# Attention on one core: the next unit's q and k projections in three parts behind the values, the first unit's in front of a branch

## The chip, the cores and the metric

The kernel runs on one core of a Trainium2 chip as one program. The metric is device time in microseconds (us), lower is better. A core has five engines with queues of their own that run side by side and wait for each other through semaphores: TensorE (matrix products, PE in the profile; its weight loads are PEld), VectorE (DVE), ScalarE (ACT), GpSimd (POOL) and SyncE (SP), which issues the transfers.

## What is computed

The reference is a chain of eight sublayers on 64 sequences of 64 tokens with 256 features; each pair is a conditioning and a mixer, and the mixer's output is added to x:

```python
x = x + _L0_attn_ref(_L0_cond_ref(x, cond, ...), query_proj, key_proj, value_proj, output_proj)
x = x + _L0_ffn_ref(_L0_cond2_ref(x, cond, weight), ...)
x = x + _L1_attn_ref(_L1_cond_ref(x, cond, Wx, Wh, b), ...)
x = x + _L1_ffn_ref(_L1_cond2_ref(x, cond, ...), Wg, W1, W2, W3)
```

The change touches the first line alone: a conditioned scan, and behind it a softmax attention inside each sequence with 16 heads of key width 16 and value width 64.

## The kernel before

The program is a row of stages on the same engines: the conditioned scan, attention, a quantised feed-forward (`ffn0`), a recurrent layer (`rnn`), a selective scan (`mamba`) and two mixtures of experts. While the first stages compute, SyncE's queue fills and packs tables in device memory for the mixtures.

The scan leaves its result `cs` with 64 channels for one half of the tokens on partitions 0 to 63 and for the other half on 64 to 127. Attention never forms the scan's output projection; it is folded into the weights: `Wqkv` (L375) gives q and k, and the values are folded into the output weights, so that the "values" of a token are the 64 scan channels themselves, turned round and kept in `rows`, and the output weights are `M`. `attention` (L310) makes `M` by `value_weights` (L297), loads a number that says whether a bias of the output projection is other than zero, and branches on it (L323, L324). The branch's body computes the bias's share with the same code; with the inputs of this case it is jumped over. Each engine passes the branch by itself, and the first instructions behind it wait for what was made in front of it. Behind the branch stands the main call of `attend`.

`attend` (L342) runs over 8 units of 512 tokens (256 of each half). A unit has four steps, for `i` in 0, 1 and `h` in 0, 1, each with 2 sequences of one half. It uses these pieces:

- `project(u, v, i)` (L369): with `i` 0 it makes q of unit `u`, with `i` 1 k. Four products go to two banks of PSUM, the memory that TensorE writes (the trace has two matmul rows for each product of this type, so eight). Then ScalarE reads them out. For q these are 16 activations (L382), since the heads of a bank are separated by four masks; for k four (L379).
- `scores(v, h, i)` (L390): products of k and q into two banks (L399), on VectorE a maximum (L404) and its subtraction (L405), on ScalarE the exponential E (L411), on VectorE its sum (L413) and reciprocal (L414), on GpSimd the scaling (L415).
- `values` (L418): products of E with `rows` into two banks (L424), and two copies to `oT` on ScalarE (L426).
- `project_out` (L428): a generator in four pieces of four products of `oT` and `M` (L433), with an addition to x on VectorE behind each second piece (L437).

PSUM in this stage is four names (`ps`, `s`, `acc`, `out`) of two banks each. A name's bank is given again when its reader is done with it, so the k projection can only be made when ScalarE has read q out of the `ps` banks.

`follow` (L444) makes one piece of an earlier unit's output and the values of an earlier step; with three steps in `late`, values run two steps behind scores. The loop at L455 sets the order: the scores of the step, one piece of other work, the next unit's q (second step) and k (third step), and `follow`. The "other work" is `keys`, which fills `rows` by 16 transposes and four copies on ScalarE (L331 to L336), then the ternary weights of `ffn0`, made on VectorE in pieces of up to 2.68 us (L511 to L518), a few squares and sums, and last a reciprocal square root (L100). The first unit's q and k are made behind the branch, before the loop.

A scheduler of the language lays each engine's instructions in an order of its own near that of the code, so a lump of activations can be split round an exponential; within an engine they then run strictly in that order.

Of the kernel before, what the change touches and what calls it, by code (L numbers as in the profile page):

```python
# [13 lines left out]
F32 = mybir.dt.float32  # L14
BF16 = mybir.dt.bfloat16
I32 = mybir.dt.int32
AF = mybir.ActivationFunctionType
# [4 lines left out]
P = 128  # L22
B, L, D = 64, 64, 256
NT = B * L
CH = 512
# [42 lines left out]
@contextmanager  # L68
def pairs_of_banks(g):

    before = g.psum
    with g.tc.tile_pool(name="pairs", bufs=2, space=PSUM) as g.psum:
        yield
    g.psum = before


def bank(g, shape=(P, CH), dt=F32, tag="ps"):
    tag = g.tag or tag
    return g.psum.tile(list(shape), dt, tag=tag, name=tag)
# [28 lines left out]
def evict(nc, i, out, in_):  # L108

    if i % 2:  # L110
        nc.scalar.copy(out, in_)
    else:
        nc.vector.tensor_copy(out, in_)
# [183 lines left out]
def value_weights(g, w, v, out, scale=1.0):  # L297


    nc = g.nc  # L300
    for i in range(0, w.H // 2, 2):
        ps = bank(g, (P, 2, D), tag="acc")
        for j in range(2):
            for r in range(2):
                rows = slice(r * L, (r + 1) * L)
                nc.tensor.matmul(ps[rows, j, :], v(i + j, rows), w.Wout[rows, i + j, :], start=True, stop=True)
        nc.vector.tensor_scalar(out[:, i : i + 2, :], ps, scale, None, ALU.mult)


def attention(g, wa, cs, beside, close_banks):  # L310

    nc, tc = g.nc, g.tc
    cs2 = cs.rearrange("p b l -> p (b l)")
    p_keys, close_keys = scoped(tc, "keys")
    M = p_keys.tile([P, wa.H // 2, D], F32, name="M")
    rows = p_keys.tile([P, NT // CH, 2, P], F32, name="keys")  # L320
    value_weights(g, wa, lambda i, r: wa.Wv[r, i, :], M)
    close_banks()
    (some,) = nc.values_load_multi_w_load_instructions(wa.any, min_val=0, max_val=D)[1]  # L323
    with tc.If(some > 0), tc.tile_pool(name="bias", bufs=1) as kp:  # L324
        ones = kp.tile([P, P], F32, name="ones")
        nc.vector.memset(ones, 1.0)
        c = kp.tile([P, wa.H // 2, D], F32, name="c")
        bv = lambda i, r: wa.bv[r, i : i + 1].to_broadcast([L, L])
        attend(g, wa, cs2, lambda u, i: ones, c, iter([lambda: value_weights(g, wa, bv, c, 1.0 / L)]), [])

    def keys():  # L331
        for i in range(NT // CH // 2):
            ps = bank(g, (P, 2, 2, P), tag="acc")
            for j in range(4):
                nc.tensor.transpose(ps[:, j // 2, j % 2], cs2[:, ts(i * 4 + j, P)], g.ident)
            evict(nc, 1, rows[:, ts(i, 2)], ps)  # L336

    attend(g, wa, cs2, lambda u, i: rows[:, u, i], M, chain((keys,), beside[0]), beside[1])
    close_keys()


def attend(g, wa, cs2, keys, M, beside, last):  # L342

    nc, tc = g.nc, g.tc
    H = wa.H
    HK = H * wa.K
    UT = CH // 2  # L350
    UB = CB // 2
    NU = NT // CH
    xh = g.xT.rearrange("p k (h t) -> p k h t", h=2)
    half = lambda i: slice(i * L, (i + 1) * L)
    with (
        tc.tile_pool(name="at2", bufs=2) as p2,
        tc.tile_pool(name="at3", bufs=3) as p3,
        pairs_of_banks(g),
    ):

        def unit():
            v = SimpleNamespace()

            v.q = p2.tile([P, 2, 2, UB, 4, L], F32, name="q")
            v.k = p2.tile([P, 2, 2, UT], F32, name="k")
            v.o = p2.tile([P, H // 2, 2, UT], F32, name="oT")
            return v

        def project(u, v, i):  # L369

            ps = [bank(g, (P, 2, UT)) for _ in range(2)]
            for hg in range(2):
                for h in range(2):
                    W = wa.Wqkv[half(h), i * HK + hg * P : i * HK + (hg + 1) * P]
                    nc.tensor.matmul(ps[h][:, hg, :], W, cs2[half(h), ts(u, UT)], start=True, stop=True)  # L375
            for h in range(2):
                for hg in range(2):
                    if i:
                        nc.scalar.activation(v.k[:, hg, h, :], ps[h][:, hg, :], AF.Identity, bias=wa.bqk[:, 1, hg : hg + 1])  # L379
                        continue  # L380
                    for j in range(4):
                        nc.scalar.activation(  # L382
                            v.q[:, hg, h, :, j, :],
                            ps[h][:, hg, :].rearrange("p (b l) -> p b l", l=L),
                            AF.Identity,
                            bias=wa.bq[:, hg, j : j + 1],
                            scale=wa.mask[:, j : j + 1],
                        )

        def scores(v, h, i):  # L390

            E = p3.tile([P, H, L], F32, name="E")
            mx = p2.tile([P, H], F32, name="mx")
            ps = [bank(g, (P, 2, 4, L), tag="s") for _ in range(2)]
            for hg in range(2):
                for r in range(2):
                    for j in range(2):
                        b = i * 2 + j
                        nc.tensor.matmul(  # L399
                            ps[r][half(j), hg], v.k[half(r), hg, h, ts(b, L)], v.q[half(r), hg, h, b], start=True, stop=True  # L400
                        )
            for r in range(2):
                m = mx.rearrange("p (hg r i) -> p r hg i", r=2, i=4)[:, r]
                nc.vector.tensor_reduce(m, ps[r], AX.X, ALU.max)  # L404
                nc.vector.tensor_tensor(  # L405
                    E.rearrange("p (hg r i) n -> p r hg i n", r=2, i=4)[:, r],
                    ps[r],
                    m.unsqueeze(3).to_broadcast([P, 2, 4, L]),
                    ALU.subtract,
                )  # L410
            nc.scalar.activation(E, E, AF.Exp)  # L411
            z = p2.tile([P, H], F32, name="z")
            nc.vector.tensor_reduce(z, E, AX.X, ALU.add)  # L413
            nc.vector.reciprocal(z, z)  # L414
            nc.gpsimd.tensor_mul(E, E, z.unsqueeze(2).to_broadcast([P, H, L]))  # L415
            return E

        def values(u, v, h, i, E):  # L418
            ps = [bank(g, (P, H // 2, L), tag="acc") for _ in range(2)]
            Er = E.rearrange("p (o r) n -> p r o n", r=2)  # L420
            s = keys(u, i)
            for r in range(2):
                for j in range(2):
                    nc.tensor.matmul(ps[j][half(r)], s[half(j), half(h)], Er[half(j), r], start=True, stop=True)  # L424
            for j in range(2):
                nc.scalar.copy(v.o[:, :, h, ts(i * 2 + j, L)], ps[j])  # L426

        def project_out(u, v):  # L428

            for k in range(KD):  # L430
                ps = bank(g, (P, 2, UT), tag="out")
                for o in range(H // 2):
                    nc.tensor.matmul(ps, M[:, o, ts(k, P)], v.o[:, o], start=(o == 0), stop=(o == H // 2 - 1))  # L433
                    if o == H // 4 - 1:
                        yield
                x = xh[:, k, :, ts(u, UT)]
                nc.vector.tensor_add(x, x, ps)  # L437
                yield


        late = []
        out = deque()

        def follow():  # L444
            for _ in islice(chain.from_iterable(out), 1):
                pass
            u, v, h, i, E = late.pop(0)
            values(u, v, h, i, E)
            if h and i:
                out.append(project_out(u, v))  # L450

        nxt = unit()
        for i in range(2):
            project(0, nxt, i)
        for u in range(NU):  # L455
            now, nxt = nxt, unit() if u + 1 < NU else None
            for i in range(2):
                for h in range(2):
                    late.append((u, now, h, i, scores(now, h, i)))
                    for piece in islice(beside, 1):  # L460
                        piece()
                    if nxt and i != h:
                        project(u + 1, nxt, i)
                    if len(late) > 2:
                        follow()
        for piece in chain(beside, last):
            piece()
        while late:
            follow()
        for _ in chain.from_iterable(out):  # L470
            pass
# [1610 lines left out]
```

## Time and profile before

| what | value |
|---|---|
| median of 10 runs | 2931.24 us (2927.79 to 2934.86) |
| profiled execution | 2930.42 us, its span 2928.5 us |
| TensorE busy | 2435.9 us, 83% of the span |
| VectorE, ScalarE, GpSimd busy | 60%, 48%, 45% |
| mean granted clock of TensorE | 0.909 |
| attention, from the branch to its last product | about 147 to 425 us |

The profile is one execution. A timeline lists instructions by start, with consecutive ones of a kind merged: the time beside the start is from the first one's start to the last one's end, `x8` is the number of rows, and the brackets hold the idle time of the engine before them and whose work ended it. A windows view gives busy time by engine in a stretch and the clock that TensorE was granted in it (1.00 is full speed).

Around the branch, VectorE writes the last part of `cs` from 146.20 to 146.89 us. Inside attention the busy times of 150 to 412 us are, on ScalarE, 60.1 us for the 128 activations of q, 34.7 us for the 64 copies to oT, 34.5 us for the 32 exponentials and 14.2 us for the 32 of k; on VectorE, 41.4 us for the subtractions, 41.1 us for the maxima, 39.0 us for the sums; on GpSimd, 61.6 us for the scaling.

### The profile page before, as it was taken

Reading aid. Unit: us, or ns where it says so; the run is one execution under the profiler, and the core shown is the slowest. Engines: PE = TensorE matmul, PEld = TensorE weight load, DVE = VectorE, ACT = ScalarE, POOL = GpSimd, SP = SyncE. Lnnn points to the kernel's source line nnn. Section 1 sums busy time; section 2 is a strip of 40 time slices with the busy share of each in tenths; the row PEclk is TensorE's granted clock in tenths of the full one; section 3 lists DMA queues with packets and bytes.
Section 4 is the critical chain, followed back from the end, with each engine's and each line's share of the span. In section 5 each row is a group of like instructions: output and inputs, shape, how many; then the busy total and the mean of one; then the engine's idle time right before and its main releaser. Section 6 shows DMA issues by size and latency. Waiting matters only on the chain.

```text
span 2928.5 us, 34738 instructions
## 1 busy us (share of the span) xinstructions
PE 2435.9 (83%) x12134; PEld 1716.6 (59%) x12148; DVE 1758.1 (60%) x2955; ACT 1413.7 (48%) x2406; POOL 1306.6 (45%) x1117
## 2 busy tenths in 40 slices
PE   4879997778857778888788888868987899999996
PEld 4533334447624455555455555546865678888885
DVE  0555547882169988898987879894344343323332
ACT  1465627774367575858465666643322222222220
POOL 0022225541067677777667777772745451111110
PEclk9978997889666999999999999989999999999998
DMA  9999610001021212121211222222786856555655
GB/s 232 367 363 340 207 25 8 19 22 55 15 65 65 79 62 76 62 76 62 76 55 69 80 76 84 79 94 68 228 281 215 309 203 247 205 204 186 221 184 181
DMA packets 183075, 406.04 MB, mean 139 GB/s; under 512 B 25312, under 2 KB 89056, under 8 KB 177520
## 3 DMA queue, kind: packets, MB, share of 16 engines
q1 hardware_dynamic: 169456, 366.80, 37.2%
q0 software_dynamic: 13440, 36.98, 3.3%
q8 instruction: 97, 1.59, 0.2%
q14 instruction: 82, 0.67, 0.1%
HBM read 280.76 MB, written 144.98 MB: 145 GB/s over the span
## 4 chain that ended last, share of the span: by engine, by line
PE 43%; DVE 19%; ACT 9%; issue 7%; POOL 5%; DMA 2%; SPq 0%; DVEq 0%; POOLq 0%; ACTq 0%
DVE hb L1000 11%; PE ps L1586 11%; PE acc L1484 7%; DVE hb L1002 3%; PE ps L1553 2%; PE yp L1016 2%; PE mq L1722 2%; PE mq L1738 2%; PE mp L897 2%; DVE xc L842 1%; PE ps L736 1%; PE ps L619 1%; POOL hb L961 1%; PE acc L736 1%; PE ps L1594 1%
## 5 line engine op out<-in xcount | busy, mean ns | idle before, releaser
L961 POOL TENSOR_TENSOR hb<-dx,Bn 128x1024 f32<-128x1024 f32 x256 | 601.6, 2361 | 261.6 <-PE yp L1016 255.1
L1000 DVE TENSOR_TENSOR_SCAN hb<-dA,hb 128x512 f32<-128x512 f32 x512 | 602.8, 1209 | 32.7 <-ACT dA L968 30.2
L968 ACT ACTIVATE dA<-delta,A 128x504 f32<-128x504 f32 x512 | 344.3, 683 | 305.4 <-DVE hb L1000 302.7
L1016 PEld LDWEIGHTS yp<-ident,hb 128*128 128x128 f32 x2048 | 268.0, 152 | 182.3 <-issue 143.8
L1002 DVE TENSOR_TENSOR hb<-hb,cb 128x1024 f32<-128x1024 f32 x256 | 312.1, 1219 | 83.0 <-PE cb L913 66.1
L1586 PE MATMUL ps<-gxT,w 128*128 128x256 f32 (+1 forms) x1600 | 325.1, 362 | 0.8 <-DVE gxT L1461 0.8
L1586 PEld LDWEIGHTS ps<-gxT,w 128*128 128x128 f32 x1600 | 276.9, 191 | 47.0 <-issue 12.1
L1016 PE MATMUL yp<-ident,hb 128*128 128x128 f32 x2048 | 302.2, 292 | 0.0
L1722 PE MATMUL mq<-x,moe_s 128*128 128x256 f32 x896 | 248.8, 410 | 49.1 <-ACT up L1729 28.4
L1268 POOL DMA_INDIRECT ffn_y<-gy,to x72 | 69.4, 964 | 457.7 <-ACT gy L1486 445.7
L1722 PEld LDWEIGHTS mq<-x,moe_s 128*128 128x128 f32 x896 | 168.2, 203 | 113.7 <-ACT up L1729 37.1
L1590 DVE TENSOR_TENSOR gh<-gs,ps 128x256 f32<-128x256 f32 (+1 forms) x200 | 78.8, 394 | 220.0 <-ACT gs L1589 219.7
L913 PE MATMUL cb<-parts,pick 80*128 80x512 bf16 x256 | 105.4, 412 | 112.6 <-DVE hb L1002 97.5
L1484 PE MATMUL acc<-w,gh 128*128 128x256 f32 (+1 forms) x864 | 187.6, 387 | 0.0
L1589 ACT ACTIVATE gs<-ps 128x256 f32<-128x256 f32 (+1 forms) x200 | 72.6, 363 | 232.4 <-PE ps L1586 227.1
L1486 ACT ACTIVATE gy<-acc,wt 128x256 f32<-128x256 f32 x152 | 67.1, 473 | 241.0 <-PE acc L1484 231.5
L415 POOL TENSOR_TENSOR E<-E,z 128x1024 f32<-128x1024 f32 x32 | 61.6, 1926 | 244.7 <-DVE z L414 169.4
L1484 PEld LDWEIGHTS acc<-w,gh 128*128 128x128 f32 (+1 forms) x864 | 145.6, 189 | 29.9 <-issue 12.8
L433 PE MATMUL out<-oT,M 128*128 128x512 f32 x256 | 129.8, 655 | 1.5 <-ACT oT L426 1.5
L1738 PE MATMUL mq<-moe_s,sh 128*128 128x256 f32 x448 | 116.7, 399 | 6.6 <-ACT up L1729 6.6
L1268 POOL DMA_INDIRECT moe_y<-gy,to x80 | 77.2, 966 | 82.0 <-ACT gy L1486 63.3
L1738 PEld LDWEIGHTS mq<-moe_s,sh 128*128 128x128 f32 x448 | 83.8, 197 | 42.5 <-issue 20.3
(462 smaller groups left out, 4506.2 us busy)
## 6 DMA issues: line engine op xcount, KB each, us to landing
w<-ffn_w SPq DMA_DIRECT2D x40, 2176.0 KB, 9.1
Bn<-B SPq DMA_DIRECT2D x128, 512.0 KB, 3.7
moe_x<-fill SPq DMA_DIRECT2D x130, 260.0 KB, 5.6
ffn_x<-fill SPq DMA_DIRECT2D x129, 260.0 KB, 5.9
w<-moe_w SPq DMA_DIRECT2D x48, 512.0 KB, 4.8
ffn_w<-in_ffn_W_dram SPq DMA_DIRECT2D x16, 640.0 KB, 8.9
gx<-moe_x SPq DMA_DIRECT2D x32, 260.0 KB, 4.9
gx<-ffn_x SPq DMA_DIRECT2D x32, 260.0 KB, 9.2
```

The lines of the kernel that those rows point to most:

```text
L433: nc.tensor.matmul(ps, M[:, o, ts(k, P)], v.o[:, o], start=(o == 0), stop=(o == H // 2 - 1))
L913: nc.tensor.matmul(t, pick[:, n : n + 1].to_broadcast([rows, P]), v.parts, start=True, stop=True)
L961: nc.gpsimd.tensor_mul(hb, vs[c].dx[p], Bn[:, n % NB, :].unsqueeze(1).to_broadcast([P, PI, CH]))
L968: nc.scalar.activation(decays[s][i][:, :, 1:], seq(vs[c].delta[p][:, i, :])[:, :, 1:], AF.Exp, scale=w.A[:, p * PI + i, n : n + 1],)
L1000: ins = nc.vector.tensor_tensor_scan(h, dA[i].rearrange("p b l -> p (b l)"), h, 0.0, ALU.mult, ALU.add)
L1002: ins = nc.vector.tensor_tensor(hb, hb, cb.unsqueeze(1).to_broadcast([P, PI, CH]), ALU.mult)
L1016: nc.tensor.matmul(yp[i][:, t, :], hb[:, i, ts(t, P)], g.ident, start=(n == 0 and t == 0), stop=(n == S - 1 and t == CH // P - 1), is_tran ...
L1268: i = self.g.nc.gpsimd.indirect_dma_start(out=self.y, out_offset=bass.IndirectOffsetOnAxis(ap=to, axis=0), in_=y, in_offset=None)
L1484: nc.tensor.matmul(po[s], h, w, start=(i == 0), stop=(i == n - 1))
L1586: nc.tensor.matmul(ps[:, j, :], v.w12[:, k, ts(j * (full + 1) + i, P)], v.xT[:, k, :], start=(k == 0), stop=(k == KD - 1))
L1722: nc.tensor.matmul(ps[:, i % 2, :], w[:, k, ts(i, P)], xu[:, k, :], start=(k == 0), stop=(k == KD - 1))
L1738: nc.tensor.matmul(ps[:, t, :], h[:, i, ts(t, P)], self.s2[:, i, :], start=(i == 0), stop=(i == NS - 1))
```

## The change

`project` and the unit's tiles become functions of their own. `project` takes a `part`: 0 makes q of the first group of heads, 1 q of the second, 2 makes k. Parts 0 and 1 each take two banks and use half of each. In the loop a part stands behind `follow`, in steps one, two and three of a unit. The tiles of q and k are two fixed sets in the outer pool in place of a rotating pair. The first unit's three parts and the filling of `rows` move in front of the branch; the branch's body, where it is taken, makes the first unit's parts again at its end. The other pieces of work each come one step earlier, since `keys` is no longer one of them.

```diff
     rows = p_keys.tile([P, NT // CH, 2, P], F32, name="keys")
+    units = [unit(p_keys, i) for i in range(2)]
+    for part in range(3):
+        project(g, wa, cs2, 0, units[0], part)
     value_weights(g, wa, lambda i, r: wa.Wv[r, i, :], M)
+    for i in range(NT // CH // 2):
+        ps = bank(g, (P, 2, 2, P), tag="acc")
+        for j in range(4):
+            nc.tensor.transpose(ps[:, j // 2, j % 2], cs2[:, ts(i * 4 + j, P)], g.ident)
+        evict(nc, 1, rows[:, ts(i, 2)], ps)
     close_banks()
...
+def project(g, wa, cs2, u, v, part):
...
+    i = part // 2
+    groups = range(2) if i else (part,)
+    ps = [bank(g, (P, 2, UT)) for _ in range(2)]
+    for hg in groups:
+        for h in range(2):
+            W = wa.Wqkv[half(h), i * HK + hg * P : i * HK + (hg + 1) * P]
+            nc.tensor.matmul(ps[h][:, hg, :], W, cs2[half(h), ts(u, UT)], start=True, stop=True)
...
         for u in range(NU):
-            now, nxt = nxt, unit() if u + 1 < NU else None
+            now, nxt = SimpleNamespace(**vars(units[u % 2])), units[(u + 1) % 2]
+            now.o = p2.tile([P, H // 2, 2, UT], F32, name="oT")
             for i in range(2):
                 for h in range(2):
                     late.append((u, now, h, i, scores(now, h, i)))
                     for piece in islice(beside, 1):
                         piece()
-                    if nxt and i != h:
-                        project(u + 1, nxt, i)
                     if len(late) > 2:
                         follow()
+                    if u + 1 < NU and i * 2 + h < 3:
+                        project(g, wa, cs2, u + 1, nxt, i * 2 + h)
```

## The prediction

> **What bounds the kernel now.** I read the page first. The program is a row of stages, and attention is the stretch from 150 to 425 us. Its rows in the costliest groups are small, so I asked for that stretch alone. The groups of TensorE there show 116.5 us of output products (L433), 51.6 us of value products (L424), 48.7 us of scores (L399) and 36.5 us of projections (L375), and TensorE is busy 28 to 30 of every 32 us: it sets the stage, ahead of VectorE (17 to 20 of 32) and ScalarE (18). The chain of waits has 32 L433 rows from 411.50 and then the next stage, with no transfer between: what attention saves should reach the end. The order of instructions behind attention is the same in both kernels.
>
> TensorE's timeline shows how a unit is lost (start, duration, engine, line, and in brackets the idle time before and who ended it):
>
> ```profile
> 228.78 1.04 PE L399 MATMUL s<-q,k 64*64 64x256 f32 x16
> 230.55 1.13 PE L375 MATMUL ps<-cs,Wqk 64*128 64x256 f32 x4 [0.73 <-ACT q L382]
> 234.19 2.07 PE L375 MATMUL ps<-cs,Wqk 64*128 64x256 f32 x4 [2.52 <-ACT q L382]
> 236.20 1.96 PE L424 MATMUL acc<-E,keys 64*64 64x512 f32 x2
> 238.09 6.31 PE L433 MATMUL out<-oT,M 128*128 128x512 f32 x8
> ...
> 373.87 3.70 PE L433 MATMUL out<-oT,M 128*128 128x512 f32 x8
> 377.50 1.09 PE L424 MATMUL acc<-E,keys 64*64 64x512 f32 x8
> 378.41 1.04 PE L399 MATMUL s<-q,k 64*64 64x256 f32 x16
> 379.38 3.70 PE L433 MATMUL out<-oT,M 128*128 128x512 f32 x8
> ```
>
> The k projection (L375 at 230.55 and 234.19) waits for ScalarE to read the q projection out of its two banks. Behind the wait the same eight L433 rows take 6.31 us and not 3.70. ScalarE's timeline says why it is late:
>
> ```profile
> 228.58 5.56 ACT L382 ACTIVATE q<-ps,bq,mask 128x256 f32<-128x256 f32 x12
> 233.97 1.14 ACT L426 COPY oT<-acc 128x512 f32<-128x512 f32 x2
> ```
>
> All 16 q activations of a unit stand in one lump (7.4 us), inside one step of 5.5 us. The windows show the second loss (columns: window, its length, busy PE, PEld, DVE, ACT, POOL, granted clock, DMA share, GB/s):
>
> ```profile
> 228.00:232.00 4.00, 2.95 (x28) 1.35 (x27) 3.23 (x6) 4.00 (x9) 1.08 (x1) 1.00 0.96 357
> 232.00:236.00 4.00, 1.80 (x4) 1.16 (x4) 1.08 (x2) 4.00 (x10) 0.82 (x1) 0.64 0.97 361
> 236.00:240.00 4.00, 4.00 (x6) 1.16 (x6) 1.47 (x2) 1.52 (x3) 1.43 (x1) 0.50 0.86 319
> 240.00:244.00 4.00, 4.00 (x7) 1.51 (x5) 0.00 (x0) 0.00 (x0) 0.47 (x1) 0.58 1.03 384
> 244.00:248.00 4.00, 4.00 (x27) 1.80 (x27) 1.69 (x3) 1.07 (x2) 0.00 (x0) 1.00 1.03 383
> ```
>
> Once TensorE has waited, its granted clock is 0.50 to 0.64 for some 10 us. Without projections (373.87 on) a step repeats every 5.51 us at clock 1.00.
>
> **The change, part by part.** A unit has four steps; a step is one call of scores, one output piece (4 products, 3.63 us from start to next start), one value call (0.91) and the next scores (0.97): 5.51 together.
>
> *Projections in three parts behind the values.* Nothing is added or removed. At full clock eight L375 rows (257.23 to the next start at 258.30) cost 1.07 us, so a q part of four rows costs 0.53 and k 1.07. A unit without waits is 4 x 5.51 + 0.53 + 0.53 + 1.07 = 24.2 us. Before, units took 34.3, 34.5, 31.8, 30.0 and 31.4 us (L433 starts at 211.92, 246.21, 280.66, 312.46, 342.46, 373.87).
>
> Is the wait really gone? ScalarE per q step: 8 x 0.463 (16 in 7.41 at 154.29) = 3.7, E 0.96, two copies to oT 0.95 to 1.07: 5.7 us against TensorE's 6.04. Its order in the changed program is q x8, E, oT x2. If a part's products end at t, oT of that step ends about t + 0.7, q about t + 4.4, and the next part wants its second bank at t + 5.5: 1.1 us to spare. E then ends at t + 5.4, is summed (1.2), inverted (0.25) and normalised on GpSimd (1.9) by t + 9, and is wanted two steps later. VectorE needs 4 x 0.62 + 1.21 + 0.25 + half of 0.65 = 4.3 us per step. So TensorE sets the pace, and the cover of ScalarE's work is 0.3 us per q step: next in line is ScalarE. The values also stay in one run of eight (1.09), where two of them alone took 1.96.
>
> From the first output piece (203.66) to the 22nd (373.87) it was 170.2 us. Now: rest of unit 1 6.58 + 5.51, units 2 to 5 4 x 24.2, three steps of unit 6 6.04 + 6.04 + 6.58: 127.4. That is **-42.8**. One step has the piece of rsqrt on ScalarE (two table loads of 1.28 and 0.42) and a product that needs a bank of the projections: between 0 and 3 us, I take 2. So **-40.8**. From piece 22 on (51.6 us to 425.5) nothing changes but one wait of 0.31.
>
> [...]
>
> *First unit's q, k and the keys in front of the branch.* Before:
>
> ```profile
> L324 ACTq EVENT_SEMAPHORE  x1: 17/17/17, 145.7 to 145.7; - x1
> L324 DVEq EVENT_SEMAPHORE  x1: 21/21/21, 150.6 to 150.6; - x1
> ...
> 150.79 2.08 PE L375 MATMUL ps<-cs,Wqk 64*128 64x256 f32 x8 [9.32 <-DVEq L324]
> 154.29 7.41 ACT L382 ACTIVATE q<-ps,bq,mask 128x256 f32<-128x256 f32 x16
> 163.74 1.98 PE L399 MATMUL s<-q,k 64*64 64x256 f32 x16
> ```
>
> (the L324 rows are of the line's own view, the others of the timeline). VectorE passes the branch last, at 150.6, and scores start 13 us later. Now ScalarE's order puts 16 q, 4 k and 4 keys behind its last logarithm (end 142.67; the M evictions move behind the scan on VectorE, which frees up to 1.6 us: 141.1). 7.4 + 1.9 + 2.4 = 11.7 gives 152.8; the passage took 145.7 - 142.67 = 3.0 us; scores start about 156.2: **-7.5**. TensorE's part there (transposes that wait for the M evictions, k behind q) ends before ScalarE's. ScalarE is then the last at the branch; -9 if its queue fills the gaps, -4.5 if the k products at half clock (2.07) and keys hold it up.
>
> *From the first scores to the first output piece:* 39.9 us before, with VectorE nearly full: six steps of 3.95 and 6.3 us of weight pieces, at least 32.2 us with the 2.2 at the start: floor -7.7. The other end is +2 (five q activations and a table load of 1.28 stand ahead of the first E). VectorE's waits of 1.27, 1.09 and 1.53 there followed products now gone or split: I take **-4**.
>
> **Sum.** -7.5 - 4 - 40.8 = -52.3 us. The profiled execution took 2930.4 us, 1.9 of it outside the span; 2930.4 - 52.3 = 2878.1. The median, 2931.2, is 0.8 above: **2879**.
>
> **The rivals.**
> *ScalarE sets the step.* For it: 5.7 of 6.04 leaves little, and its q rows have a median of 582 ns each where they are not packed. 8 x 0.582 + 2.03 = 6.7: 0.65 over, twice a unit, and each unit keeps a spell of half clock. The best unit before (30.0) lost 30.0 - 24.2 - 2.0 = 3.8 beyond its wait. A unit is then 29.3, 5.1 more, times 127.4/24.2 = 5.3: 27 us given back, **2905**. Against: packed rows cost 0.46.
>
> *Only the waits go.* If the half clock has its own rhythm, the gain between pieces is the idle time alone: 0.73 + 2.52 + 2.06 + 2.44 + 2.01 + 2.02 = 11.8. 2930.4 - 7.5 - 4 - 11.8 + 2 = 2909, **2909**. [...] Against it: clock 1.00 between the spells, and each spell begins at a wait.
>
> *Slower: the clock stays half.* Short waits can also do it:
>
> ```profile
> 189.54 1.08 PE L399 MATMUL s<-q,k 64*64 64x256 f32 x8 [0.47 <-DVE E L405]
> 191.77 1.61 PE L424 MATMUL acc<-E,keys 64*64 64x512 f32 x4 [0.52 <-POOL E L415]
> ```
>
> and 192 to 196 had clock 0.57. If each of the steps that now hold a part brings such a wait, the products stay slow through the stage. With the 11.5 us saved ahead, the change loses from 1 + f = (170.2 + 11.5 - 2)/127.4, f = 0.41 of the work at half clock. With two thirds of it there it is 212 + 2 against 170.2, less 11.5: +32, **2963**. Against: 216 to 228 and 244 to 264 hold clock 1.00 with scores, values, a projection and output in a row.
>
> *It does nothing:* the parts wait as before and the branch costs what it saves: **2931**. The order of the changed program speaks against it.
>
> **How the numbers follow.** Forecast 0.69, ScalarE 0.12, only the waits 0.10, half clock 0.06, nothing 0.03. The forecast's own ends are -9 - 7.7 - 42.8 = -59.5 (2872 by the median) and -4.5 + 2 - 39.8 = -42.3 (2889). The range takes in these and the first two rivals, and a few us more below for the free rhythm of the clock: 2867 to 2910. A measurement of this kernel can tell about 0.2% (6 us) from no change. Faster 0.91, same 0.03, slower 0.06.
>
> **What would show it.** L433 starts 24 us apart from unit to unit; no wait of a projection for ScalarE over 0.5 us; clock near 1.00 from the third unit on; first scores at about 156 and first output at about 192; end of attention near 373. Units of 29 with waits would mean ScalarE; no waits and clock 0.5, the last rival but one; scores later than 163, a branch costlier than read.

## The result

| what | before | changed |
|---|---|---|
| median | 2929.63 us (31 runs, 2916.57 to 2936.10) | 2885.19 us (9 runs, 2875.69 to 2892.73) |
| profiled execution, its span | 2930.42, 2928.5 | 2887.62, 2885.9 |
| mean granted clock of TensorE | 0.909 | 0.914 |
| first scores | 163.74 us | 157.76 us |
| first output product | 203.66 us | 197.22 us |
| 22nd output piece | 373.87 us | 331.76 us |
| last run of output products starts | 411.50 us | 369.40 us |

The ratio is 0.9842 (95% interval 0.9829 to 0.9855): 46 us faster by the ratio, 44 by the medians. The forecast was 2879, so the sign and the mechanism held, and the sum was some 6 us too good by the median, 10 by the two traces. In these two traces nearly all of it arises in attention: the last run of output products starts 42.1 us earlier and the span is 42.6 shorter.

Lines have moved in the changed kernel: scores are L410, projections L366, the q activations L373, values L435, copies to oT L437, output products L444 and the branch L332. TensorE's timeline of the changed kernel, in unit 4 (counted from 0, as in the prediction):

```profile
262.68 3.70 PE L444 MATMUL out<-oT,M 128*128 128x512 f32 x8
266.31 1.09 PE L435 MATMUL acc<-E,keys 64*64 64x512 f32 x8
267.33 0.70 PE L366 MATMUL ps<-cs,Wqk 64*128 64x256 f32 x4
267.96 1.09 PE L410 MATMUL s<-q,k 64*64 64x256 f32 x16
```

No row carries a bracket: TensorE waits for nothing here, and eight output rows take 3.70 us in every piece of the settled units. ScalarE's timeline of the same place:

```profile
268.65 3.77 ACT L373 ACTIVATE q<-ps,bq,mask 128x256 f32<-128x256 f32 x8
272.25 1.11 ACT L422 ACTIVATE E<-E 128x1024 f32<-128x1024 f32 x1
273.76 1.07 ACT L437 COPY oT<-acc 128x512 f32<-128x512 f32 x2 [0.39 <-PE acc L435]
```

The lump of 16 is two of 8 (the second starts at 274.72) with an exponential and two copies between them, in the order that the prediction counted on. The windows of the changed kernel (columns as in the prediction) give the stretch from the scores to the first output product and one whole unit:

```profile
157.76:197.22 39.46, 32.80 (x173) 15.28 (x173) 27.88 (x42) 27.45 (x51) 9.16 (x5) 0.67 1.02 373
262.68:287.55 24.87, 24.87 (x149) 10.03 (x145) 17.83 (x28) 17.18 (x34) 7.61 (x4) 1.00 0.94 315
```

The unit takes 24.87 us, TensorE is busy in all of it, and the clock is 1.00; the unit from 211.38 on is the same. The one between them takes 26.44, since it holds the piece of the reciprocal square root. The first row is the weak place: 0.67. In front of it stands the branch (the ScalarE row is from the timeline, the first from the branch line's own view, the last from TensorE's timeline):

```profile
L332 ACTq EVENT_SEMAPHORE  x1: 17/17/17, 157.7 to 157.7; - x1
...
144.61 7.39 ACT L373 ACTIVATE q<-ps,bq,mask 128x256 f32<-128x256 f32 x16 [4.33 <-DVE cs L218]
...
157.76 1.99 PE L410 MATMUL s<-q,k 64*64 64x256 f32 x16 [4.74 <-ACTq L332]
```

ScalarE is now the last at the branch, as forecast, but its q begins at 144.61, not 141.1: it waits for VectorE's last write of the scan.

### The profile page after: what moved, and what is told of

Same layout as the page of the kernel before. It is cut to its first block, busy times and chain, and to the rows that moved or that the text cites. A ratio compares the mean times of both kernels' runs of the same rounds, so it can differ in the third digit from the quotient of the medians.

```text
span 2885.9 us, 34737 instructions
## 1 busy us (share of the span) xinstructions
PE 2413.2 (84%) x12134; PEld 1706.7 (59%) x12148; DVE 1756.9 (61%) x2955; ACT 1412.0 (49%) x2406; POOL 1305.5 (45%) x1117
## 4 chain that ended last, share of the span: by engine, by line
PE 44%; DVE 19%; ACT 9%; issue 7%; POOL 4%; DMA 3%; SPq 0%; DVEq 0%; POOLq 0%; ACTq 0%
DVE hb L1009 11%; PE ps L1595 11%; PE acc L1493 8%; DVE hb L1011 3%; PE ps L1562 2%; PE yp L1025 2%; PE mq L1731 2%; PE mq L1747 2%; PE mp L906 2%; DVE xc L851 1%; PE ps L745 1%; PE ps L628 1%; POOL hb L970 1%; PE acc L745 1%; PE ps L1603 1%
## 5 line engine op out<-in xcount | busy, mean ns | idle before, releaser
L444 PE MATMUL out<-oT,M 128*128 128x512 f32 x256 | 119.6, 612 | 1.5 <-ACT oT L437 1.5
```

## The experiments

Twelve runs, in four groups; kernels of a group shared a chip and the runs of the kernel before. The chips differ: the first group's took 2981.44 us for the kernel before, the others 2923.75 to 2928.39. So totals are compared inside a group. The changed kernel itself was measured on two occasions, 0.9842 and 0.9888, where 0.984 was expected again; the two intervals do not meet, so what the change is worth differs by some 0.4% with the chip or the occasion. Between groups I compare times inside attention, which repeat: scores of the changed kernel start at 157.76 and 157.78 us in two traces on two occasions, and the 24.87 us of a unit is the same in both. Behind attention, single traces of these kernels on the faster chips differ by up to some 8 us (2516 to 2525 us from the last run of output products to the end, once 2506), which no theory here is about. So what attention saves need not all show in the total: in the second trace of the changed kernel that run starts at 366.13, 45.4 us before the 411.50 of the kernel before (traced on another occasion), and its median is 35.5 us below that of the kernel before on the same chip.

The theory: TensorE's waits for ScalarE's lump, and the half clock behind each wait, cost about 41 us in the loop; the front brings the rest. Three columns are read from every trace: first scores, from there to the first output product, and the length of a settled unit; the unit with the reciprocal square root, 26.3 to 31.4 us, is left out of it, except for the kernel before and the front alone. Each row stands on one trace.

| kernel | ratio to before (95%) | first scores | to first output | a unit |
|---|---|---|---|---|
| before | 1 | 163.74 | 39.92 | 30.0 to 34.5 |
| changed | 0.9842 (0.9829 to 0.9855) | 157.76 | 39.46 | 24.87 |
| loop alone | 0.9874 (0.9845 to 0.9904) | 159.74 | 32.72 | 24.87 |
| front alone | 0.9947 (0.9929 to 0.9965) | 157.96 | 39.95 | 28.2 to 31.5 |
| lump, steps two and three, behind | 0.9897 (0.9876 to 0.9919) | 157.76 | 34.71 | 26.44 |
| three parts, ahead | 0.9890 (0.9868 to 0.9913) | 158.09 | 43.28 | 24.4 to 24.8 |
| lump, steps one and three, behind | 0.9940 (0.9917 to 0.9964) | 157.11 | 36.61 | 27.4 to 29.1 |
| one mask of four, loop of before | 0.9850 (0.9824 to 0.9876) | 155.25 | 33.75 | 24.18 |
| twelve activations for each q part | 0.9899 (0.9871 to 0.9926) | 160.04 | 40.55 | 26.4 |
| changed, again | 0.9888 (0.9867 to 0.9909) | 157.78 | 37.87 | 24.87 |
| loop alone, again | 0.9880 (0.9859 to 0.9901) | 159.72 | 34.57 | 24.87 |
| keys behind the branch | 0.9893 (0.9871 to 0.9915) | 154.81 | 45.44 | 24.9 |
| keys behind, unit tiles apart | 0.9867 (0.9843 to 0.9892) | 157.38 | 41.71 | 24.9 |
| filler | 0.9880 (0.9859 to 0.9900) | 157.95 | 38.54 | 24.87 |

### The loop alone, and the front alone

The first kernel keeps the changed loop and puts the first unit's parts and the keys back behind the branch:

```diff
-    for part in range(3):                           # ahead of the branch
-        project(g, wa, cs2, 0, units[0], part)
-    for i in range(NT // CH // 2): ...              # keys, ahead of the branch
...
+        for part in range(3):                       # behind it
+            project(g, wa, cs2, 0, units[0], part)
-        attend(..., M, *beside)
+        attend(..., M, chain((keys,), beside[0]), beside[1])
```

> The loop of the changed kernel; the first unit's q, k and the keys behind the branch as before. My theory (the lump of q keeps its two banks too long, TensorE waits, and each wait brings a spell of half clock): nearly all of the gain is here. Units 24.9 us apart, no wait of a projection over 0.5 us in units 2 to 6, first scores at about 163.7; 2893 us, 37 below the kernel before. Rival (the gain is the start in front of the branch and shorter work there): units as before, 2923.

The second keeps the front and takes the old loop:

```diff
+                    if u + 1 < NU and i != h:
+                        project(g, wa, cs2, u + 1, nxt, 2 if i else 3)   # 3: both groups of q
                     if len(late) > 2:
                         follow()
-                    if u + 1 < NU and i * 2 + h < 3:
-                        project(g, wa, cs2, u + 1, nxt, i * 2 + h)
```

> The first unit's q, k and keys in front of the branch; the loop of before (q in one lump in step two, k in step three, both ahead of the values). My theory: first scores at 157.8, units of 30 to 34.5 us as before, 6 us gained: 2923. Rival: over 20 us gained, because a changed start also shifts where the spells of half clock fall.

Measured: 0.9874, or -37 us on 2981, as expected, for the loop; 0.9947, or -16 us, for the front, where I expected 6 and the rival over 20. The front alone saves 5.8 us up to the scores and nothing up to the first output; its other 12 us lie behind, where its units take 30.7, 28.2, 30.0, 30.0 and 31.5 us (before 34.3, 34.5, 31.8, 30.0 and 31.4). They have the old loop's waits, most of them 2.0 us, but fewer products at half clock behind them: from the first to the 22nd output piece the mean granted clock is 0.93, where the kernel before has 0.87. So a changed start does shift the spells, as the rival said. Why they fell as they did I can't show; what the traces say of when a spell begins stands at the end of the section on the prediction.

What I had not expected is in the first kernel's third column: behind the branch, the scores start 2 us later than in the changed kernel and the first output comes 4.8 us earlier (192.46; in the second pair of traces 1.4 earlier).

### Which part of the loop does it

Lump in steps two and three as before, but behind the values:

```diff
                     if len(late) > 2:
                         follow()
+                    if u + 1 < NU and i != h:
+                        project(g, wa, cs2, u + 1, nxt, 2 if i else 3)
```

> The changed kernel, but q is made in one part (step two) and k in step three, both behind the values. My theory: place does not help, distance does. k wants the second bank about 6 us after q's products, ScalarE is done with 16 activations after 8.1: a wait of about 2 us in every unit, and the spell of half clock behind it; units of 29 to 33, 2905 to 2915. Rival (the order behind the values, which keeps the value products in one run, is what counts): units of 24.6, 2883.

Three parts, but ahead of the values:

```diff
+                    if u + 1 < NU and i * 2 + h < 3:
+                        project(g, wa, cs2, u + 1, nxt, i * 2 + h)
                     if len(late) > 2:
                         follow()
```

> The changed kernel, but the three parts stand ahead of the output piece and the values, as the projections did before. My theory: the distance of one step is kept, so waits stay under 0.5 us and units near 25 to 25.5; 2888. Rival (the place behind the values counts): values are broken up again, units of 28 to 30, 2905.

Lump in step one and k in step three, behind the values:

```diff
                     if len(late) > 2:
                         follow()
+                    if u + 1 < NU and not h:
+                        project(g, wa, cs2, u + 1, nxt, 2 if i else 3)
```

> The changed kernel, but q is made in one part in step one and k two steps later, in step three, both behind the values. My theory (distance between a projection and the next user of its banks): about 12 us lie between, ScalarE needs 8.1: no wait, clock 1.00, and one run of eight products less to set up: units of 24.6, 2883, the same as the changed kernel. Rival (the split itself is needed, because E stands behind 16 activations): values wait for E, units over 27, 2898 or more.

The three parts ahead of the values have settled units of 24.38 us, 0.5 shorter than the change's own: the split alone takes the waits away, the place behind the values is not needed. Its total (-33 us by the ratio) is short of the -41 that I expected, as its first steps took 43.3 us; its last run of output products starts at 369.23, the changed kernel's at 369.40. (The totals of the loop alone, of this kernel and of the next have intervals that overlap; the traces tell them apart.) The lump behind the values keeps a wait. TensorE's timeline of that kernel:

```profile
277.52 1.13 PE L366 MATMUL ps<-cs,Wqk 64*128 64x256 f32 x6 [1.25 <-ACT q L373]
```

It is 1.25 us a unit; the eight value rows ahead of it (1.09 us) and the six behind it (1.13) have the length of the changed kernel's at clock 1.00, and the unit is 26.44: most of the gain is there too. I put that down to k being asked for later, behind the step's values: the wait was 2.0 to 2.5 us before. The total, -31 us by the ratio, lies between the two expectations.

The lump two steps ahead of k was a miss: 0.9940 where I expected the whole gain. The projection waits for nothing there, but something else is late. ScalarE's and TensorE's timelines of that kernel:

```profile
297.82 7.39 ACT L373 ACTIVATE q<-ps,bq,mask 128x256 f32<-128x256 f32 x16
305.01 1.14 ACT L422 ACTIVATE E<-E 128x1024 f32<-128x1024 f32 x1
305.96 1.16 ACT L437 COPY oT<-acc 128x512 f32<-128x512 f32 x2
```

```profile
307.17 2.44 PE L444 MATMUL out<-oT,M 128*128 128x512 f32 x4 [2.84 <-ACT oT L437]
```

Behind 16 activations, the exponential and two copies to oT end at 307.1, and the output products wait 2.84 us for them, once in most units (2.90 in the first). The clock does not stay whole either: behind this wait and the one at 336.28 the eight output rows took 5.40 and 5.17 us instead of 3.70 (granted clock 0.80 over 8.43 us and 0.82 over 8.21), behind the one at 279.75 they did not (1.00 over 6.74). The lump that step one asks for is read out in step two, where the values that complete a unit's oT are made (at 302.37), and the next output piece reads them at once. So the lump itself is the cost: in the three places tried here one of ScalarE's readers waits behind it, and only splitting it removed that.

### Less and more work on ScalarE

One mask of four in the old loop (heads of the other three masks have q set to zero once, so a part of the computation is left out):

```diff
-            for j in range(4):
+            for j in range(1):      # q activations; the old loop, and the front of the changed kernel
```

> The loop of before with the start of the changed kernel, and q made for one of its four masks alone: 4 activations a unit instead of 16; the other three quarters of q are zeros, so the scores of three heads in four are left out in value, not in work. My theory (waits for ScalarE bring the half clock): TensorE's program is that of e2, the waits are gone, and with them the spells: units of 24.2 to 25, clock 1.00, about 2882. Rival (the half clock has its own rhythm): no waits but spells of 0.5 for some 8 us in each unit, units of 28 to 30, about 2905.

Twelve activations in each q part in place of eight (four are repeated):

```diff
-            for j in range(4):
+            for j in (0, 1, 2, 3, 0, 1):
```

> The changed kernel with 12 activations in each q part instead of 8 (two masks are written twice with the same values). ScalarE then needs 12 x 0.463 + 2.0 = 7.6 us in a q step where TensorE needs 6.3. My theory: TensorE waits about 1.3 us twice a unit and the clock halves behind it: units of 31 to 33, 2915 to 2925. Rival (waits this short do not touch the clock): units of 27.5, 2897.

With a quarter of the masks the old loop runs without a wait. The windows of that kernel:

```profile
246.05:270.24 24.19, 24.19 (x149) 10.42 (x145) 17.16 (x28) 12.11 (x21) 8.66 (x5) 1.00 0.97 359
```

The same products, with the projections in their old place, and the half clock is gone with the waits. TensorE's order is not quite that of the kernel before, though: there k's eight rows stand in two runs of four and the values of that step in runs of two, three and three, and here both are whole, which is worth some 2 us a unit by itself (shown below). From the first to the 22nd output piece it takes 129.6 us; the forecast's sum for a loop without waits was 129.4. So without the waits there is no half clock in the loop, as the theory has it, and the total (-44 us) is what it gave. That a wait brings it also where nothing else in TensorE's order is broken up, the lump in steps one and three shows: its outputs at 5.40 and 5.17 us stand behind a wait of 2.84, with values and projections in whole runs.

With twelve activations a part, units take 26.4 us, and the total, 2898.30, is the rival's and not the theory's. TensorE waits 0.2 us in a few places (0.21 at 280.36, 0.19 at 282.27), and the rows round them show no half clock: eight of values take 1.09 us and 16 of scores 1.09, as in the changed kernel at 1.00. ScalarE is busy 20.5 of 26.4 us. The eight activations that were added cost 1.5 us a unit, no spell. Most of it is no wait either: TensorE's own rows take 26.05 us where they took 24.87, as k's eight take 1.96 instead of 1.14 and q's second four 1.12 instead of 0.70. These waits of 0.2 us did not bring the clock down.

### Where the front's gain went

Now the changed kernel and three neighbours on one chip.

> The changed kernel once more, as the measure for the three kernels beside it on the same chip. 0.984 of the kernel before; in its trace first scores at about 157.8 us, first output product at about 197, the last run of output products (x32) starts at about 369.

> Only the loop is changed; the first unit's q and k and the keys stay behind the branch, as before. Its trace of the first run has first scores at 159.7 us, 2.0 later than the changed kernel, but the first output product at 192.5, 4.8 earlier, and the last output products at 364.2 against 369.4. Theory (moving the front ahead of the branch empties TensorE around the branch, so that it comes to the scores at half clock, waits there for ScalarE and stays at half clock until 174; behind the branch the keys and projections keep it busy and the clock is back at 164): about 5 us faster than the changed kernel on the same chip, 0.9825 of the kernel before. Rival (the front was worth its 6 us, and the first run's 0.987 says so): 6 to 9 us slower than the changed kernel, 0.987.

The third has only the keys back behind the branch, as the first piece of the loop:

```diff
-    for i in range(NT // CH // 2): ...              # keys, ahead of the branch
-        attend(g, wa, cs2, units, lambda u, i: rows[:, u, i], M, *beside)
+        attend(g, wa, cs2, units, lambda u, i: rows[:, u, i], M, chain((keys,), beside[0]), beside[1])
```

> The changed kernel, with only the keys (16 transposes on TensorE, 4 copies on ScalarE) back behind the branch, as the first piece of the loop. ScalarE comes to the branch 2.2 us earlier: first scores at about 155.6 instead of 157.8, by both theories. Theory (TensorE lacks work behind the branch): the transposes fill its gaps, its clock is back at 1.00 some 13 us after its first work instead of 17 and with no second half-clock spell, and from scores to the first output product it takes 33 to 35 us instead of 39.5, so first output at about 190 and 6 to 8 us less than the changed kernel in all. Rival (the four copies on ScalarE, 2.4 us, cost behind the branch what they save ahead of it): first output at 196 to 198, total within 2 us of the changed kernel.

The fourth has the same and its q and k tiles in a pool on the other side of memory:

```diff
-    units = [unit(p_keys, i) for i in range(2)]
+    p_units, close_units = scoped(tc, "units", side="right")
+    units = [unit(p_units, i) for i in range(2)]
```

> As the kernel with the keys behind the branch, and the two units' q and k tiles in memory of their own, that the scan's pools do not use. Theory (ScalarE's first q waits until 144.6 for VectorE's last write of the scan into memory that q takes over): first q at 141 to 142, scores at about 153.5, 2 to 3 us less in all than the kernel beside it. Rival (q waits for something else, or VectorE, which ends its M copies at 147.1, is last at the branch): no change within 1 us.

Medians: changed 2888.26, loop alone 2885.92, keys behind 2888.52, keys behind with tiles apart 2881.14 us, against 2923.75. The loop alone is not slower than the whole change: moving the front brought nothing that can be measured. The rival (6 to 9 us slower) falls. The theory expected 5 us in favour of the loop alone; 2.3 were measured: the intervals of the ratios overlap, the six runs of each hardly do (2884.69 to 2887.40 and 2887.27 to 2889.64). In the traces attention ends at the same time in both (the last run of output products starts at 365.99 and 366.13), so the 2.3 us are no proof of the theory.

The windows of the changed kernel's second trace, from scores to the first output, and of the two traces of the loop alone:

```profile
157.78:195.65 37.87, 31.85 (x173) 14.47 (x173) 27.93 (x42) 27.93 (x51) 9.50 (x5) 0.70 1.01 367
```

```profile
159.74:192.46 32.72, 27.67 (x173) 14.04 (x173) 26.86 (x40) 27.16 (x53) 7.81 (x5) 0.84 0.99 362
```

```profile
159.72:194.29 34.57, 29.34 (x173) 14.32 (x172) 26.83 (x40) 27.14 (x53) 7.80 (x5) 0.77 1.00 364
```

As many TensorE rows, 173, stand in all of them (in the loop alone eight are transposes of the keys, and eight rows of scores come later); the stretch is longer where the granted clock (third number from the end) is lower, also between two executions of one kernel: 32.72 at 0.84, 34.57 at 0.77, 37.87 at 0.70, 39.46 at 0.67. In the changed kernel TensorE has nothing to do from 153.0 to 157.8, comes to the scores at half clock, and stays there until about 174; with the front behind the branch it works through from 149 on with gaps of about 0.5 us, is at half clock at the scores too, and has clock 1.00 and 0.84 from 164 to 168 in its two traces.

That fits "the branch starves TensorE", but the third kernel contradicts the simple form of it. Its scores came at 154.81, 3 us earlier, the clock was back at 158 already, and then:

```profile
164.08 0.70 PE L369 MATMUL ps<-cs,Wqk 64*128 64x256 f32 x2 [1.44 <-ACT q L376]
```

```profile
164.90:178.00 13.10, 13.10 (x42) 5.51 (x44) 5.79 (x10) 7.65 (x15) 3.26 (x2) 0.50 0.98 360
```

Behind the second q part's wait of 1.44 us the clock fell, and TensorE was busy for 13.1 us on end at 0.50. A second such spell ran from 189 to 209. First output: 200.25, where 190 was expected. This trace is of the slowest of that kernel's six runs (2900.13 us; four of them lie between 2887.6 and 2888.8), so such spells are not the rule there; but the median, 2888.52, is also the changed kernel's and not 6 to 8 us below it. In all four kernels activations of unit 1's first q part stand on ScalarE ahead of the first exponential, and the second part waits for its banks (1.94 us in the changed kernel, at 167.01); the first steps have too little else to cover it.

The tiles apart did not do what they were for: q waited for VectorE's last write all the same, and the scan itself ended later (q at 148.02). So that it waits for memory of the scan's pools is not borne out. It waits for the write of `cs` in any case. VectorE's four evictions of `M` run between the scan's last steps there (from 140.53 to 143.81), where in the changed kernel they follow it (from 144.60), which fits the later end. That kernel's 7 us below the changed one lie behind attention: its last run of output products starts no earlier (370.79), and from there to the end it takes 2506 us, the changed kernel's second trace 2522.

### Filling TensorE's gaps

```diff
+                    if u * 4 + i * 2 + h < 6:
+                        for _ in range(2):
+                            ps = bank(g, (P, 4, P), tag="acc")
+                            for j in range(4):
+                                nc.tensor.transpose(ps[:, j], cs2[:, ts(j, P)], g.ident)
                     if len(late) > 2:
                         follow()
```

> The changed kernel with work added: in each of the first six steps of attention, eight transposes of the input into banks that nobody reads (48 in all, 128x128, 0.12 us each at full clock and 0.24 at half), behind the scores and ahead of the values and the projection. First scores stay at 157.8. Theory (what the first unit loses is TensorE's clock: it was busy 2.1 to 2.9 of 4 us there and its mean clock was 0.67 and 0.70 in the two traces of the changed kernel, 0.77 and 0.84 in the two traces with the front behind the branch, and the shorter way to the first output product went with the higher clock each time): with its gaps filled the clock rises by 168 and holds, mean 0.85 or more, and the first output product comes at 190 to 193 instead of 195.7 to 197.2, although 6 to 10 us of work were added; the total is 3 to 6 us below the changed kernel, ratio 0.983 if before is as in the first comparison. Rival (the clock in these steps does not follow TensorE's gaps, or VectorE and ScalarE set the pace there whatever the clock): the mean clock stays at or below 0.75, the added work comes on top, first output at 200 to 205, total 4 to 8 us above the changed kernel.

The first output came at 196.49, between the two expectations, and the total is 0.9880 (2893.36 against 2928.39). The windows of that kernel, up to 178 us and from there on:

```profile
157.95:178.00 20.05, 18.06 (x91) 9.67 (x92) 10.76 (x17) 10.73 (x20) 1.90 (x1) 0.59 1.03 381
178.00:196.49 18.49, 18.08 (x129) 9.32 (x129) 16.27 (x24) 13.39 (x25) 7.15 (x4) 1.00 1.00 365
```

From 178 on, with hardly a gap (18.08 of 18.49 busy), the clock holds 1.00, where the changed kernel's first trace has a second spell, from 180 to 191; its second trace holds 1.00 from 180 to 188 and has 0.82 and 0.76 in the two stretches of 4 us behind. Ahead of 178 a gap of 1.99 us at 165.3 remained, and 10 us at half clock followed (0.50 from 168 to 176, 0.79 from there to 180). Over the whole stretch the mean is 0.79, below the 0.85 of the theory and above the 0.75 of the rival. So gaps and spells go together here too, but the filler costs about what it saves, and it doesn't settle what the stretch would take at full clock.

## Why the prediction was right, and where it was off

**The waits go, and the half clock with them: right.** The projection's waits for ScalarE of up to 2.5 us are gone (none over 0.31 in units two to six), the clock is 1.00 in them, and units fell from 30.0 to 34.5 to 24.87 us. The kernels with one mask and with the lump in steps one and three show that the waits brought the half clock, and the loop alone that the loop carries the gain. But not all of the loss was one or the other, as the prediction's rivals have it (3.8 us beyond the wait in the unit of 30.0). TensorE's timeline of that unit in the kernel before:

```profile
330.06 1.13 PE L375 MATMUL ps<-cs,Wqk 64*128 64x256 f32 x4
333.20 1.13 PE L375 MATMUL ps<-cs,Wqk 64*128 64x256 f32 x4 [2.01 <-ACT q L382]
```

Two runs of four rows take 1.13 and 1.06 us (the second up to the next row's start) at full clock, where eight in one run take 1.07; and the values, laid in runs of two, three and three round this wait, take 1.0 us more than in one. So the unit is 24.2 us, 2.0 of wait, 2.1 of broken runs and 1.7 of half clock (its eight output rows took 5.40). My estimate for the whole stretch, 40.6 us longer than with one mask: some 12 of waits (the prediction's 11.8), 22 of half clock (the mean clock is 0.87 over 170.2 us) and 10 of broken runs, some 3 too many in all.

**First to 22nd output piece: -35.7 and, in the second trace, -37.4 (132.85 us), against -40.8.** Three sizes were off. A unit is 24.87 and not 24.2: four rows that stand alone take 0.63 from start to start and not 0.53, they start 0.1 later behind the values, and the scores take a little longer, so a q step is 6.31 instead of 6.04 and the k step 6.73 instead of 6.58. Over five and a half units that is 3.5 us. The first piece still ran at half clock: its step was 2.1 us longer in the profiled execution, 1.7 of it in the eight output rows. The rsqrt piece cost 1.56, where I took 2.

**First scores -6.0, against -7.5.** q waited until 144.61 for the scan's last write, which I had left out: 3.5 us late. Its q, k and keys then took 10.8 us instead of 11.7, and from there (155.40) to the scores it was 2.4, not 3.4. But the loop alone, with the front behind the branch, already has -4.0: TensorE's first product behind the branch comes at 149.06 instead of 150.79 there, and the scores 10.7 us later instead of 13.0.

**From scores to the first output -0.5 (second trace -2.1), against -4: the step that failed.** I summed VectorE's work and let the waits shrink. What sets this stretch, by the four windows above, is TensorE's clock behind the branch and behind the wait for the second q part, and the front made the first of these worse. That is as far as it is known: the kernel with the keys behind the branch and the filler did not come out as this account had it. Scores and this stretch together gained 6.4 and 8.0 us with the front moved, 11.2 and 9.4 without it: my sum of 11.5 was nearly met by the kernel that leaves the front where it was, which is chance.

**What attention saves should reach the end.** It did in the first pair of traces (42.1 and 42.6 us). In the second trace of the changed kernel attention ends 45.4 us earlier than in the kernel before and the total fell by 35.5; where the rest went is not shown.

**Rivals.** ScalarE does not set the step: four more activations in each of two parts (3.7 us a unit) lengthened a unit by 1.5, so over 1 us in each q step was still covered, not 0.3. "Only the waits go" (2909) is refuted by the clock of the units and by the kernel with one mask; but that the half clock has something of a rhythm of its own holds, as follows. That the clock stays half never came near in the loop; in the first steps it is what happens (0.50 from 156.50 to 173.57 in the changed kernel's first trace).

**When the clock fell, and when it came back.** It fell in or behind gaps of 1.44, 1.99 and 2.5 us. Behind a gap of 1.25 us in the lump-behind kernel the rows kept the length that they have at 1.00, and gaps of 2.84 in the two-step kernel lowered it only in some units (0.80 and 0.82 in the 8 us behind, or 1.00). It came back at different times too: the 1.5 us lost behind such a gap there are about 3 us at half clock, but 13.1 us of unbroken work ran at 0.50 in the kernel with the keys behind. And the same stretch of one kernel differs from execution to execution: 0.67 and 0.70, 0.84 and 0.77 in the two pairs of repeated traces.

In the traces of the kernel before and of the changed kernel, every change of the granted clock falls on one grid of 3.41 us, which lies elsewhere in each (a change at 233.14 us in the first, at 200.88 in the second): windows asked for on it, from 158 to 376 and from 146 to 365 us, show 0.50 or 1.00 and nothing between. The half-clock spells in attention there last 3.41, 6.83, 10.24 and, once, 17.07 us. The windows view of the kernel before, asked for on its grid:

```profile
229.73:233.14 3.41, 1.22 (x8) 0.67 (x4) 3.35 (x7) 3.41 (x9) 1.90 (x1) 1.00 0.95 353
233.14:236.55 3.41, 2.35 (x5) 1.45 (x6) 0.00 (x0) 3.41 (x8) 0.00 (x0) 0.50 1.00 370
...
243.38:246.79 3.41, 3.41 (x27) 1.47 (x26) 0.48 (x1) 1.07 (x2) 0.00 (x0) 1.00 1.03 386
```

TensorE was busy for 1.22 us of a window of the grid, and at its end the clock fell, while the wait (231.7 to 234.2) still lasted. So the length of a wait alone does not say what follows it; where it lies in the grid differs too. In the kernel with the lump in steps one and three, whose clocks behind its waits fit a grid of the same step, 2.84 us left 1.50 us of a window busy where the clock held (277.84 to 281.25) and 1.39 where it fell (305.15 to 308.56). The busy time of a window does not tell the two apart either, as the clock also fell behind one with 2.34 us busy (332.13 to 335.54, kernel before).

The experiments point to the loop's change without the front's, and to a projection ahead of the values (24.38 us a unit); the two together were not run. Open are also how little work in a window brings the half clock, how many windows it then lasts, and the 7 us behind attention in the kernel with tiles apart.

## What to carry to other kernels

A lump of small readers on one engine was late for someone in each place where it was put: moving it changed who waited (k's banks, 1.25 us, or the output's oT, 2.84), and only splitting it into pieces shorter than a step took the wait away. Waits of 1.4 to 2.5 us on TensorE were mostly followed here by 3.4 to 13.7 us at half clock, once by some 20 (189 to 209 with the keys behind), which loses half of that, so count it as part of a wait's price (one of 1.86 us, at 182.71 there, was followed by none up to 188); and look whether the products round the wait are laid in broken runs, which cost as much as the wait here. And work that is moved ahead of a barrier is not saved just because the barrier opens earlier: here scores that came 2 us earlier were lost again before the first output. Look at what the move leaves behind.

## What was not expected of the hardware

- TensorE ran at clock 0.50 for 13.1 us without a gap (164.90 to 178.00 in the kernel with the keys behind), and for 9.2 us in the kernel before (234.19 to 243.38); behind waits of 2.84 us it was back after some 3.4 (0.80 over 8.43 us). Every change in the traces of the kernel before and of the changed kernel came on a grid of 3.41 us.
- The same program has different clocks in one stretch from execution to execution: 0.84 and 0.77 over about 33 us, which is 1.9 us of time.
- A branch whose body is jumped over took ScalarE 3.8 us from its compare (153.9) to the release behind it (157.7), 2.3 of them after its last copy had ended; TensorE's weight loads were in it for 4.3 us (149.3 to 153.7).
